# A graph layer on one core: setup, end of the kernel, order of the one-hots and shares of the gather changed

## The chip, the core and the metric

The kernel runs on one core of a Trainium2 chip. The core has TensorE (PE; its weight loads are shown apart as PEld), VectorE (DVE), ScalarE (ACT), GpSimd (POOL) and SyncE (SP), each with an instruction stream of its own that is worked off in order, and 16 DMA engines that all of them feed. The metric is the time of one execution on the device in microseconds (us); lower is better. Before the change the median of three runs is 1567.36 us (1563.31 to 1572.13).

## The reference

A layer of a graph network: 6250 nodes with 64 features, 200,000 edges sorted by destination.

```python
w = silu(edge_attr @ W1 + b1) @ W2 + b2              # (E,32)@(32,64), then @(64,9)
h_src = features[src]                                # a row of x for every edge
msg = einsum('ef,em,fmg->eg', h_src, edge_sh * w, W_tp)   # f=64, m=9, g=64
agg = segment_sum(msg, dst, num_segments=N) / sqrt(16)
emb = silu(c_noise[:, None] @ Wn1 + bn1) @ Wn2 + bn2
gamma, beta = split(emb, 2, axis=-1)
x = layernorm(x + agg * (1.0 + gamma) + beta)
```

All in float32.

## The kernel before

Edges are cut into 1563 tiles of 128 (one edge to a partition), the tiles into 98 groups of 16 (`KB`; the last has 11). The nodes make 49 columns of 128 (`NJ`).

**Rows of x for the edges.** A tile's 128 rows of x come in one of three ways. Most tiles are gathered by GpSimd, one indirect DMA a tile (`gather`, L91), into `hs`, of which there are seven buffers (`AHEAD` + 1). The last three or four tiles of each group are "picked" on TensorE (`pick`, L463 to L486): x lies in SBUF as two parts (`xs`, a rounded one and the rest) in 7 x 128 rows of 7 nodes; `hots` (L460, VectorE) makes a one-hot matrix of the tile's keys, `hot_k`, and 14 matmuls of 128 x 448 (L475) choose blocks of seven rows into `px` (two buffers); two VectorE operations (`xm`, L484 and L486) choose the row out of the seven. `picked(g)` says how many of a group are picked: 355 in all. The keys are worked out once in the setup on VectorE, transposed, written to DRAM (`kd`), and loaded for two groups at a time spread over all partitions (`load_keys`, `kr`, L391); `keys` (L454, ScalarE) puts them into PSUM. In every sixth group from 7 (`SPG`, 16 groups) the first tile's rows are loaded by SyncE one row at a time (`load_rows`, L101 and L106): it reads 8 row numbers into registers and issues 8 DMAs of 256 bytes, 22 rows (`SPR`) in a turn, beginning six turns ahead.

**Messages.** For each group `hidden` (L403, L411) and `second` (L420, L423) are the two layers on the edge attributes, `weights` (L430 to L442) forms `a`, the weights spread over a window of eight nodes. `windows` (L504, L514) multiplies the rows of x with `a` per tile into sums for eight nodes; `project` (L543, L546, L549) multiplies them by `W_tp` for a pair of groups; `place` (L559) puts them on node columns with a one-hot matrix, adding the part that the column before carried over (`carry`, `yt`); `bring` (L576) transposes two columns, and `finish` does the residual, the scale and shift and the layer norm (L669 to L682) and stores them (L683). `gate` (L589, L355, L356) makes the scale and the shift of one column a turn, up to turn 50.

**The order** is written out by hand (`tc.manual_schedule`); each engine keeps the order in which the program issues. A turn i of the main loop works on several groups at once: it gathers group i + 6, loads edge data and keys, issues SyncE's rows, makes the one-hots of group i + 2 (`hots(i + 2, 0, 2)`, then `hots(i + 2, 2, Q)`), picks the first tile of group i + 1 with the parts of `nodes(i)` (gate, place or bring, finish) put between its matmuls, then `hidden(i + 2)`, `second(i + 1)`, `windows(i)`, `project` in odd turns, and the other picks of group i + 1. `nodes(i)` and `second(i + 1)` share one PSUM buffer (tag `s`), so L420 of `second` must wait until everything of `nodes` is read. `project` and `hidden` share another (tag `p1`), so L543 waits until the Silu of L411 has read it. `finish` is in every fourth turn from turn 7 and needs a square root on ScalarE (L679), which loads another function table than Silu's.

**Setup** loads the indices and x, works out the keys of all groups, writes `kd` and reads it back, splits x into `xs` (`between` puts other work between the seven parts; each part goes through PSUM), spreads the first destination of every tile over the partitions with matmuls (`base`) and begins groups 0 and 1. **The end**: after the last turns the last pair and the last single group go through project, place, bring and finish separately.

Of the kernel before, what the change touches and what calls it, by code (L numbers as in the profile page):

```python
# [30 lines left out]
SPG = range(7, NBLK, 6)  # L31
SPR = 22
# [17 lines left out]
def picked(g):  # L50

    return Q - (3 * g % 8 < 3)
# [7 lines left out]
def gnn_resnorm_kernel(ctx: ExitStack, tc: tile.TileContext, x, src, dst, dst_row, ea, sh, cn,  # L60
# [18 lines left out]
    with ExitStack() as fast:  # L79
# [18 lines left out]
        def load_rows(g, e0):  # L98
            for e in range(e0, min(e0 + SPR, P), 8):
                n = min(8, min(e0 + SPR, P) - e)  # L100
                _, vs = nc.values_load_multi_w_load_instructions(  # L101
                    src_r[SPG.index(g):SPG.index(g) + 1, e:e + n], engines=[mybir.EngineType.SP],
                    min_val=0, max_val=NPAD - 1,
                    skip_runtime_bounds_check_because="src is below N, as for the gathers")
                for k in range(n):
                    nc.sync.dma_start(hs[g][e + k:e + k + 1, 0, :], x[bass.ds(vs[k], 1), :])  # L106
# [19 lines left out]
        kd = dram.tile([C, P], F16, name="kd")  # L126
        cn_d = dram.tile([P, NJ], F32, name="cn_d")
# [6 lines left out]
        def setup(temp):  # L134
# [7 lines left out]
            xb_r = xb.rearrange("p j f -> p (j f)")  # L142
            row_i = xb_r[0:1, 0:NBLK * KB].bitcast(I32)
            nc.scalar.dma_start(row_i, dst[0:1, :])
            first_i = temp.tile([NBLK, KB], I32)
            nc.scalar.dma_start(first_i, dst[0].rearrange("(g k) -> g k", k=KB))
            cn_j = temp.tile([NJ, P], F32)
            nc.scalar.dma_start(cn_j, cn)
            for s in range(2):
                nc.scalar.dma_start(b1c[s * H:(s + 1) * H, :], b1.unsqueeze(1))  # L150
# [3 lines left out]
            for h0, h1 in ((0, 2), (2, 4), (4, 7)):  # L154
                nc.scalar.dma_start(xk[:, h0:h1, :], x_v[:, h0:h1, :])
            load(0)
            for s in range(2):
                nc.sync.dma_start(w2p[s * H:(s + 1) * H, s * M:(s + 1) * M], w2)
            nc.sync.dma_start(dst_i, dst)

# [17 lines left out]
            row_f = xb_r[0:1, NBLK * KB:2 * NBLK * KB]  # L178
            nc.scalar.copy(row_f, row_i)
# [7 lines left out]
            nc.vector.tensor_add(ident2, ident[:, 0:F], ident[:, F:P])  # L187
            zero = temp.tile([P, 1], F32)
            nc.vector.memset(zero, 0.0)
            for k in range(2):  # L190
                nc.vector.memset(ht[k][H:H + 1], 1.0)
            nc.vector.memset(wtc2[F:P, 4], 0.0)
            ones1 = temp.tile([1, P], F32)
            nc.vector.memset(ones1, 1.0)
# [7 lines left out]
            s_f, kp, kh, rest, t0, t1 = [zt_r[:, k * C:(k + 1) * C] for k in range(6)]  # L202
            ti = [t.bitcast(I32) for t in (t0, t1)]
            s_f = s_f.rearrange("p (g k) -> p g k", k=Q)
            nc.vector.tensor_copy(s_f[:, 0:NBLK - 1, :],
                                  src_i.rearrange("p (g k) -> p g k", k=KB)[:, 0:NBLK - 1, KB - Q:])
            nc.vector.tensor_copy(s_f[:, NBLK - 1, :], src_i[:, NT - Q:NT])
            s_f = s_f.rearrange("p g k -> p (g k)")
            nc.vector.tensor_scalar(ti[0], s_f, 2675.0, None, op0=ALU.mult)
            nc.vector.tensor_scalar(ti[0], ti[0], 17, None, op0=ALU.logical_shift_right)  # L210
            nc.vector.tensor_copy(kp, ti[0])
            nc.vector.scalar_tensor_tensor(rest, kp, -float(J * J), s_f, op0=ALU.mult, op1=ALU.add)
            nc.vector.tensor_scalar(ti[1], rest, 37.0, None, op0=ALU.mult)
            nc.vector.tensor_scalar(ti[1], ti[1], 8, None, op0=ALU.logical_shift_right)
            nc.vector.tensor_scalar(kh, ti[1], float(P), None, op0=ALU.mult)
            kf = s_f
            nc.vector.tensor_add(kf, kp, kh)
            for c0 in range(0, C, P):
                n = min(P, C - c0)
                p_kt = psum.tile([P, P], F32, tag=("s", "r")[c0 // P % 2], name=f"p_kt{c0}")  # L220
                nc.tensor.transpose(p_kt[0:n], kf[:, c0:c0 + n], ident)
                kt = t1[:, c0 // 2:c0 // 2 + P // 2].bitcast(F16)
                nc.scalar.copy(kt[0:n], p_kt[0:n])
                nc.sync.dma_start(kd[c0:c0 + n, :], kt[0:n])
            nc.vector.scalar_tensor_tensor(jl, kh, -float(J) / P, rest, op0=ALU.mult, op1=ALU.add)
            hidden(0, act=False)
            load_keys(0)
            load_keys(LB)
# [4 lines left out]


            rel_v = rel.rearrange("p (a b c) -> p a b c", a=2, b=2)
            dst_v = dst_i.rearrange("p (a b c) -> p a b c", a=2, b=2)
            row_v = row_f.rearrange("p (a b c) -> p a b c", a=2, b=2)

            def base(a_):
                p_b = psum.tile([P, 2, KB * P // 4], F32, tag="p1", name=f"p_b{a_}")  # L240
                for b_ in range(2):
                    nc.tensor.matmul(p_b[:, b_, 0:NBLK * KB // 4], ones1, row_v[:, a_, b_, :], start=True, stop=True)
                nc.vector.tensor_sub(rel_v[:, a_], dst_v[:, a_], p_b[:, :, 0:NBLK * KB // 4])
# [17 lines left out]
            def between(h):  # L261

                if h == 0:
                    p_f = psum.tile([KB, NBLK], F32, tag="s", name="p_f")
                    nc.tensor.matmul(p_f, first_t, ident[0:NBLK, 0:NBLK], start=True, stop=True)
                    nc.scalar.copy(first_f, p_f)
                elif h == 1:
                    keys(0)
                    hots(0, 0, Q)
                elif h == 3:  # L270
                    p_cn = psum.tile([P, NJ], F32, tag="s", name="p_cn")
                    nc.tensor.matmul(p_cn, cn_j, ident[0:NJ, 0:NJ], start=True, stop=True)
                    cn_s = temp.tile([P, NJ], F32)
                    nc.scalar.copy(cn_s, p_cn)
                    nc.sync.dma_start(cn_d, cn_s)
                    nc.sync.dma_start(wn1c, wn1.rearrange("o h -> h o"))
                    nc.sync.dma_start(bn1c, bn1.unsqueeze(1))
                    gate_load(0)
                    nc.sync.dma_start(wn2a[0:H, :], wn2)
                    nc.sync.dma_start(wn2a[H:H + 1, :], bn2.unsqueeze(0))  # L280
                    for q in range(2):
                        n = (M + 1 - q) // 2
                        nc.sync.dma_start(wtc2[q * F:(q + 1) * F, 0:n, :], wtp[:, q:M:2, :])
                    load(LB)
                    with nc.allow_non_contiguous_dma(reason="2048 words, once"):
                        nc.sync.dma_start(src_r, src[:, SPG[0] * KB:NBLK * KB:6 * KB].rearrange("p g -> g p"))


            for h in range(J):
                xh = gam[:, h * J:(h + 1) * J, :].rearrange("p l f -> p f l")  # L290
                xp = psum.tile([P, F, J], F32, tag="px" if h in (2, 3) else "pz", name=f"x{h}", bufs=2)
                nc.scalar.copy(xp, xh)
                nc.scalar.copy(xs[0][:, h], xh)
                nc.vector.tensor_sub(xs[1][:, h], xp, xs[0][:, h].bitcast(F32))  # L294
                if h == 1:
                    hidden_act(0)
                between(h)
            pick(0, 0)
            keys(1)
            hots(1, 0, Q)  # L300
            base(0)
            near(0)
            second(0)
            pick(0, 1)
            base(1)

# [3 lines left out]
            for f in weights(0):  # L310
                f()
            ids()
            hidden(1)
            nc.scalar.copy(zt[F:P, :, 4].rearrange("p a k w -> p a (k w)"),
                           zero[F:P, :, None].to_broadcast([F, 4, P]))
            for t in range(2, Q):
                pick(0, t)
# [41 lines left out]

        def finish(j0, j1, sums):  # L360
            y = late.tile([P, j1 - j0, F], F32, tag="y", name=f"y{j0}")
            finish_nodes(nc, late, eps, sums, y, gam[:, j0:j1, :], xb[:, j0:j1, :], out_v[:, j0:j1, :], j0)
# [25 lines left out]
        def load_keys(g):  # L388
# [3 lines left out]
                              rows(kd[g * Q:(g + n) * Q, :].rearrange("c e -> (c e)"), P))  # L392
# [101 lines left out]
        def windows(g):  # L494
# [4 lines left out]
            for k0 in range(0, nk, ZT):  # L499
# [12 lines left out]
                for v in range(2):  # L512
                    for h in range(2):
                        nc.scalar.copy(  # L514
# [15 lines left out]
        def project(q):  # L530
# [3 lines left out]
            pt = psum.tile([P, 2, 4 * P], F32, tag="p1", name=f"pt{q}")  # L534
            z = [zs.pop(g).rearrange("p c k w -> p c (k w)") for g in gs]
            if len(gs) == 1:
                for c in range(5):
                    nc.tensor.matmul(pt[:, 0, 0:F], z[0][:, c], wtc2[:, c, :], start=(c == 0), stop=(c == 4))
                halves(q, pt[:, 0, 0:F].unsqueeze(1))
                return []  # L540
            for c in range(5):
# [12 lines left out]
        def place(q, pd):  # L554
# [3 lines left out]
            def part(k):  # L558
                nc.tensor.matmul(pd, r[q][:, k].rearrange("p s f -> p (s f)"), hot.pop(gs[k]),  # L559
                                 start=(k == 0), stop=(k == len(gs) - 1))  # L560
                if k == len(gs) - 1:
                    r.pop(q)
                    if q > 0:
                        yt[q - 1] = work.tile([P, P], F32, tag="yt", name=f"yt{q}", bufs=3)
                        nc.vector.tensor_add(yt[q - 1], pd[:, 0:P], carry.pop(q - 1))  # L565
# [34 lines left out]
        with tc.manual_schedule(), tc.tile_pool(name="temp", bufs=1) as temp:  # L600
            setup(temp)

            for i in range(NBLK):
# [34 lines left out]
                if i == NBLK - 1:  # L638
                    for f in turn:
                        f()  # L640
# [217 lines left out]
```

## Time and profile before

| | us |
|---|---|
| median of three runs | 1567.36 |
| the profiled execution, its own time | 1570.09 |
| its span | 1568.3 |
| TensorE busy | 1460.5 |
| VectorE busy | 1139.5 |
| GpSimd busy (0.3 us between its gathers not counted) | 1129.5 |
| ScalarE busy | 528.6 |
| first window matmul | 55.8 |
| last window matmul | 1551.9 |

Busy times are sums over the span; a line of a group names the line of the kernel, the engine, the operation, what is written from what, the count, then busy time, mean nanoseconds of one, and the idle time of that engine just before with what ended it. A line in order of time gives start and duration, and in brackets the wait just before it and what ended that. A line of a window gives busy time and count of PE, PEld, DVE, ACT and POOL, then the granted clock of TensorE as a share of full speed, the busy share of the DMA engines and GB/s.

### The profile page before, as it was taken

The page shows a single profiled execution, that of the slowest core. Times are in us where ns is not written, and L with a number is a line of the kernel's source. Part 1 is how long each engine was busy: PE and PEld are TensorE (multiplying, and loading weights), DVE is VectorE, ACT ScalarE, POOL GpSimd, SP SyncE. Part 2 cuts the span into 40 slices and gives each one's busy share as a digit, 9 for nine tenths or more (in the row PEclk, how much of TensorE's full clock was granted, in tenths as well). Part 3 has the DMA queues.
Part 4 walks back from the last instruction along what each step waited for, and adds up shares of the span by engine and source line. Part 5 has one row for each costly group of instructions (what it writes and reads, how often), then busy time and mean ns, then how long its engine had stood idle before and what let it go on. Part 6 is the DMA issues. An engine that isn't in the chain of part 4 may idle for free.

```text
span 1568.3 us, 34363 instructions
## 1 busy us (share of the span) xinstructions
PE 1460.5 (93%) x10810; PEld 1208.6 (77%) x10810; DVE 1139.5 (73%) x1987; ACT 528.6 (34%) x1335; POOL 1129.5 (72%) x1201
## 2 busy tenths in 40 slices
PE   4998999999999999999999999999999999999995
PEld 2787778778787788787877877877877878778774
DVE  5686777777777777777777777777777677777773
ACT  4232242433332423332333323323233332333331
POOL 7777777777777777777777777777777777777700
PEclk9999999999999999999999999999999999999997
DMA  5321222222222222222222222222222222222200
GB/s 166 93 62 55 53 75 51 63 56 71 57 62 65 63 54 61 56 71 59 58 71 53 59 53 71 59 53 70 53 60 55 68 54 58 71 53 59 71 7 5
DMA packets 90939, 96.16 MB, mean 61 GB/s; under 512 B 37161, under 2 KB 51451, under 8 KB 90748
## 3 DMA queue, kind: packets, MB, share of 16 engines
q1 hardware_dynamic: 51842, 53.09, 11.5%
q0 software_dynamic: 38144, 39.14, 11.4%
q8 instruction: 88, 1.44, 0.4%
q10 hardware_dynamic: 762, 1.64, 0.3%
q14 instruction: 103, 0.84, 0.2%
HBM read 92.04 MB, written 1.73 MB: 60 GB/s over the span
## 4 chain that ended last, share of the span: by engine, by line
PE 51%; POOL 20%; DVE 13%; issue 8%; DMA 4%; ACT 3%; SPq 0%; DVEq 0%; POOLq 0%; ACTq 0%
PE px L475 37%; POOL hs L91 20%; DVE hot_k L460 5%; PE pz L504 5%; DMA hs<-in_x_dram,src_i 4%; PE pt L543 3%; PE p L420 2%; DVE xm L484 2%; DVE hs L486 2%; PE p L403 1%; PE p L430 1%; ACT L411 1%; ACT st L411 1%; DVE oh L382 1%; ACT carry L568 1%
## 5 line engine op out<-in xcount | busy, mean ns | idle before, releaser
L91 POOL DMA_INDIRECT hs<-in_x_dram,src_i x1192 | 1128.2, 946 | 364.0 <-issue 335.0
L475 PE MATMUL px<-xs,hot_k 128*128 128x448 f32 x4970 | 1100.8, 375 | 8.4 <-DVE xs L294 7.8
L475 PEld LDWEIGHTS px<-xs,hot_k 128*128 128x128 f32 x4970 | 903.3, 190 | 96.7 <-issue 12.2
L484 DVE SCALAR_TENSOR_TENSOR xm<-li,jl,px 128x448 f32<-128x448 f32 x355 | 240.4, 677 | 220.2 <-PE px L475 217.9
L460 DVE TENSOR_TENSOR hot_k<-pk,nk 128x896 fp32r<-128x896 f32 x355 | 370.5, 1081 | 2.3 <-ACT pk L454 2.3
L486 DVE TENSOR_REDUCE hs<-xm 128x64 f32<-128x448 f32 x355 | 220.1, 620 | 12.5 <-DVE xm L484 0.2
L514 ACT COPY zt<-pz 64x160 f32<-64x160 f32 (+2 forms) x784 | 213.3, 272 | 23.0 <-PE pz L504 13.9
L411 ACT ACTIVATE st<-p,b1c 128x1024 f32<-128x1024 f32 x98 | 109.2, 1114 | 296.1 <-PE p L403 295.8
L568 ACT COPY carry<-ps 128x128 f32<-128x128 f32 x48 | 12.7, 265 | 390.2 <-DVE yt L565 382.4
L436 DVE TENSOR_TENSOR p<-p,sh 128x72 f32<-128x72 f32 x196 | 47.3, 241 | 132.7 <-ACT rt L546 47.7
L504 PEld LDWEIGHTS pz<-a,hs 128*64 128x64 f32 x3126 | 110.6, 142 | 41.9 <-issue 38.4
L442 DVE TENSOR_TENSOR a<-oh,p 128x1152 f32<-128x1152 f32 x98 | 132.6, 1353 | 3.3
L504 PE MATMUL pz<-a,hs 128*64 128x72 f32 x3126 | 125.5, 236 | 1.1 <-DMA hs<-in_x_dram,src_i 0.6
L403 PE MATMUL p<-ea,w1bd 64*128 64x512 f32 x392 | 113.5, 656 | 0.0
L420 PEld LDWEIGHTS p<-st,w2p 128*32 128x32 f32 x784 | 16.6, 108 | 113.3 <-issue 52.7
L543 PE MATMUL pt<-zt,wtc 128*64 128x128 f32 x960 | 72.8, 305 | 27.7 <-ACT st L411 26.0
L420 PE MATMUL p<-st,w2p 128*32 128x256 f32 x784 | 63.7, 395 | 35.7 <-DVE xb L356 32.0
L543 PEld LDWEIGHTS pt<-zt,wtc 128*64 128x64 f32 x960 | 62.2, 157 | 29.7 <-ACT st L411 27.8
L679 ACT ACTIVATE var<-var,eps 128x2 f32<-128x2 f32 (+1 forms) x25 | 7.4, 296 | 220.5 <-DVE var L678 220.5
L430 PE MATMUL p<-ident,p2s 128*128 128x128 f32 x196 | 54.4, 278 | 0.0
L454 ACT CAST pk<-kr 128x384 f32<-128x384 f16 (+1 forms) x98 | 53.9, 550 | 1.5 <-DMA kr<-kd 1.4
L403 PEld LDWEIGHTS p<-ea,w1bd 64*128 64x128 f32 x392 | 30.2, 188 | 28.8 <-issue 27.9
(122 smaller groups left out, 530.0 us busy)
## 6 DMA issues: line engine op xcount, KB each, us to landing
hs<-in_x_dram SPq DMA_DIRECT2D x2048, 0.2 KB
ea<-in_ea_dram SPq DMA_DIRECT2D x49, 512.0 KB
hs<-in_x_dram,src_i POOLq DMA_INDIRECT x1192
kr<-kd SPq DMA_DIRECT2D x49, 256.0 KB
sh<-in_sh_dram SPq DMA_DIRECT2D x49, 144.0 KB
cb<-cn_d SPq DMA_DIRECT2D x12, 128.0 KB
out_dram<-o SPq DMA_DIRECT2D x24, 64.0 KB
gam<-in_x_dram ACTq DMA_DIRECT2D x2, 448.0 KB
```

The costliest lines, as they stand in the source:

```text
L91: hs_dma[g] = [nc.gpsimd.indirect_dma_start(out=hs[g][:, t - g * KB, :], out_offset=None, in_=x, in_offset=bass.IndirectOffsetOnAxis(ap=sr ...
L403: nc.tensor.matmul(p1[:, i, :], w1bd[i * 64:(i + 1) * 64, :], e[i * 64:(i + 1) * 64, :], start=True, stop=True)
L411: nc.scalar.activation(st[g], p1_t.pop(g), AF.Silu, bias=b1c)
L420: nc.tensor.matmul(p2[g][c * D:(c + 1) * D, 0, :].rearrange("p (i e) -> p i e", i=2), w2p, s[:, :, c * P:(c + 1) * P], start=True, stop=True)
L442: nc.vector.tensor_mul(a[g], oh_t.pop(g)[:, :, None, :].to_broadcast([P, KB, M, W]), sw.unsqueeze(3).to_broadcast([P, KB, M, W]))
L460: nc.vector.tensor_tensor(hot_k[g, t], pk_t[g][:, t, None, :].to_broadcast([P, J, P]), nk.unsqueeze(2).to_broadcast([P, J, P]), op=ALU.is_ ...
L475: nc.tensor.matmul(px.rearrange("p f l -> p (f l)"), hot_k[g, t][:, h, :], xs[i][:, h].rearrange("p f l -> p (f l)"), start=(h == 0 and i ...
L484: nc.vector.scalar_tensor_tensor(xm, li[:, None, :].to_broadcast([P, F, J]), jl[:, c:c + 1], px, op0=ALU.is_equal, op1=ALU.mult)
L486: nc.vector.tensor_reduce(hs[g][:, tiles(g) - q + t, :], xm, AX.X, ALU.add)
L504: mm = nc.tensor.matmul(pz[v * F:(v + 1) * F, k // 2].rearrange("p m w -> p (m w)"), hsg[:, k0 + k, :], ag[:, k0 + k].rearrange("p m w -> ...
L514: nc.scalar.copy(z[h * F:(h + 1) * F, 0:5 - h, k0 + v:k0 + n:2, :].rearrange("p m k w -> p k m w"), pz[v * F:(v + 1) * F, 0:(n + 1 - v) // ...
L543: nc.tensor.matmul(pt[h * F:(h + 1) * F, 0, 0:P], wtc2[:, c, :], z[h][:, c], start=(c == 0), stop=(c == 4))
```

## The change

Eight edits:

- The setup works out and stores the keys of the first two groups alone first (`key_rows(0, LB)`, stored to `kd_0`), and those of the other 96 after two picks of group 0 (`key_rows(LB, NBLK)`).
- x is rounded and split straight from SBUF (`split`), not through PSUM, and its loads are issued ahead of two small ones.
- The first destination of each tile comes to all partitions by one DMA of 128 equal rows (`row_i`), not by one row, a cast and matmuls; `rel` is a subtraction of two SBUF tiles. The other small loads of the setup move behind the picks of group 0.
- In a turn, the first two one-hots of group i + 2 are issued behind the parts of `nodes(i)`, still between the matmuls of the first pick (`more`).
- Picked tiles: one fewer in every third group (359 in all), not in three of eight (355).
- SyncE's rows: every fifth group (19 tiles), 26 rows a turn in batches of 13.
- A store of `finish` is issued at the head of the next turn; in `place` the carry copy is issued ahead of the addition; a single group's `project` uses the PSUM tag `r`.
- The end: windows of the last group go in reverse order, half of the copies of the last two groups go to VectorE, and the last pair and the last single group share one `place`, one `bring` and one `finish` of three columns.

```diff
-SPG = range(7, NBLK, 6)
-SPR = 22
+SPG = range(7, NBLK, 5)
+SPR = 26
...
-    return Q - (3 * g % 8 < 3)
+    return Q - (g % 3 == 0)
...
-            for e in range(e0, min(e0 + SPR, P), 8):
-                n = min(8, min(e0 + SPR, P) - e)
+            for e in range(e0, min(e0 + SPR, P), SPR // 2):
+                n = min(SPR // 2, min(e0 + SPR, P) - e)
...
+            row_i = xb.rearrange("p j f -> p (j f)")[:, 0:NBLK * KB].bitcast(I32)
+            nc.sync.dma_start(row_i, rows(dst[0, :], P))
...
+            key_rows(0, LB)
+            load_keys(0)
             hidden(0, act=False)
-            load_keys(0)
-            load_keys(LB)
...
+            def split(h):
                 xh = gam[:, h * J:(h + 1) * J, :].rearrange("p l f -> p f l")
-                xp = psum.tile([P, F, J], F32, tag="px" if h in (2, 3) else "pz", name=f"x{h}", bufs=2)
-                nc.scalar.copy(xp, xh)
                 nc.scalar.copy(xs[0][:, h], xh)
-                nc.vector.tensor_sub(xs[1][:, h], xp, xs[0][:, h].bitcast(F32))
-                if h == 1:
-                    hidden_act(0)
-                between(h)
+                nc.vector.tensor_sub(xs[1][:, h], xh, xs[0][:, h].bitcast(F32))
+
+            for h in range(2):
+                split(h)
+            hidden_act(0)
+            keys(0)
+            hots(0, 0, Q)
+            for h in range(2, J):
+                split(h)
+            load(LB)
+
+            nc.vector.tensor_sub(rel[:, 0:2 * KB], dst_i[:, 0:2 * KB], row_i[:, 0:2 * KB])
+            near(0)
+            keys(1)
             pick(0, 0)
-            keys(1)
-            hots(1, 0, Q)
-            base(0)
-            near(0)
+            hots(1, 0, 2)
             second(0)
             pick(0, 1)
-            base(1)
-
+            for f in weights(0):
+                f()
+            key_rows(LB, NBLK)
+            load_keys(LB)
+            hots(1, 2, Q)
+            hidden(1)
+            for t in range(2, Q):
+                pick(0, t)
+            nc.vector.tensor_sub(rel[:, 2 * KB:], dst_i[:, 2 * KB:], row_i[:, 2 * KB:])
...
+            loads_late()
             ids()
-            hidden(1)
-            for t in range(2, Q):
-                pick(0, t)
...
                 if i + 2 < NBLK:
                     keys(i + 2)
-                    hots(i + 2, 0, 2)
-                pick(i + 1, 0, [nodes(i)])
+                    more = [lambda: hots(i + 2, 0, 2)]
+                pick(i + 1, 0, [nodes(i), more])
...
-                        nc.scalar.copy(
+                        (nc.vector.tensor_copy if v and g >= NBLK - 2 else nc.scalar.copy)(
...
+            turn = project(NBLK // 2 - 1)
             project(NBLK // 2)
+            for f in turn:
+                f()
+            ps = psum.tile([P, 2 * P], F32, tag="s", name="ps_n")
+            py = psum.tile([P, 3, F], F32, tag="r", name="py_n")
+            for f in place(NBLK // 2 - 1, ps, NBLK // 2) + bring(NJ - 3, NJ, py):
                 f()
```

`key_rows(g0, g1)` has the arithmetic that the setup had for all groups at once, on the columns of groups g0 to g1, with its transposes, copies and stores.

## The prediction

> **What bounds the kernel now.** I read the page's shares first, then TensorE's waits, then one loop turn in order of time, then the granted clock, then GpSimd's and SyncE's groups. The page:
>
> ```profile
> span 1568.3 us, 34363 instructions
> PE 1460.5 (93%) x10810; PEld 1208.6 (77%) x10810; DVE 1139.5 (73%) x1987; ACT 528.6 (34%) x1335; POOL 1129.5 (72%) x1201
> ...
> L91 POOL DMA_INDIRECT hs<-in_x_dram,src_i x1192 | 1128.2, 946 | 364.0 <-issue 335.0
> ```
>
> TensorE is busy for 93%. GpSimd's 72% hides a second bound: the gathers follow one another every 0.95 + 0.30 = 1.25 us, "issue" being no wait. From the tile view of hs, 1192 gathers from 2.9 to 1493.2 us make 1.251 us each: GpSimd never stops. Counting gathers against the starts of the window matmuls (L504), each group's last gather is done 32 us (group 3) to 56 us (groups 44 and 97) before TensorE needs it. So TensorE sets the pace, 15.33 us a turn (windows of turn 8 at 183.9, of turn 95 at 1517.2), with GpSimd close behind at 1192/98 x 1.251 = 15.22. The chain's 20% for GpSimd is an artefact: its DMA pieces lie beside ordinary 0.30 us issue gaps. What makes TensorE wait:
>
> ```profile
> PE p L420 <- DVE xb L356: 32.0, 34, 2.2
> PE pt L543 <- ACT st L411: 26.0, 12, 2.2
> ```
>
> Columns: us, times, longest. These two are nearly all the idle time of turns 0 to 95. Their cause, in turn 27 (in order of time: start, duration):
>
> ```profile
> 472.86 2.08 DVE L460 TENSOR_TENSOR hot_k<-pk,nk 128x896 fp32r<-128x896 f32 x2
> ...
> 473.08 0.33 PE L576 MATMUL ps<-ident,yt 128*128 128x64 f32 x2
> ...
> 474.86 0.28 DVE L669 TENSOR_TENSOR y<-ps,gam 128x128 f32<-128x128 f32 x1
> 475.00 1.13 PE L403 MATMUL p<-ea,w1bd 64*128 64x512 f32 x4
> ...
> 477.87 0.21 DVE L356 TENSOR_TENSOR xb<-xb,ps 128x64 f32<-128x64 f32 x1
> ...
> 478.23 0.64 PE L420 MATMUL p<-st,w2p 128*32 128x256 f32 x8 [2.10 <-DVE xb L356]
> ```
>
> The sums of two output columns are in PSUM at 473.41; VectorE takes them at 474.86, as two hot_k stand before them; the last reader of that bank (L356) ends at 478.08, and L420, which needs the bank, has waited 2.10 us. Then the clock:
>
> ```profile
> 479.60:483.00 3.40, 3.40 (x36) 3.03 (x33) 1.72 (x2) 2.81 (x11) 2.77 (x3) 0.50 0.63 218
> 1215.00:1276.00 61.00, 60.20 (x444) 50.11 (x444) 43.63 (x73) 18.79 (x53) 46.05 (x50) 0.97 0.23 59
> ```
>
> The seventh figure is the granted clock: 0.50 from 479.6 to 483.0. I found 14 such stretches between 168 and 1525 us, each beginning 2.0 to 3.8 us after the start of a stall of 2.1 to 2.2 us; 9 of the 23 such stalls had none, and no stall of 0.4 us had one. Turn 24 (half clock at 418.2) took 15.41 us, turn 16, of the same pattern but none, 13.77: one costs 1.63 us.
>
> **The change, part by part** (against the profiled execution: span 1568.3, its own time 1570.09, so 1.8 outside; the median 1567.36 is 2.7 lower).
>
> (1) First two hot_k of group i+2 behind the node work (`more`). In finishing turns (every fourth, from 7) VectorE takes the sums at about 473.6, just after TensorE wrote them, 1.26 us earlier; the chain to L356 (3.22 us) ends at 476.8, and TensorE, ready at 476.13, waits 0.8 in place of 2.1: 11 x 1.3 = 14.4. Late next are the hot_k (wanted a turn later) and xm, 1.1 us later, where VectorE had 2.7 us idle before the next L436; px has two buffers and hot_k seven, so nothing on TensorE waits. Without that cover each finishing turn pays about 1 us, 24 in all. In other turns the 0.38 waits (23) and 0.15 waits on carry (22) go: 8.8 + 3.3. From turn 51 on no gate follows, and the stall is L543 on the Silu that stands behind Sqrt and its table load; these start 1.9 us earlier (mul at 1513.75 for 1515.64), so 2.17 becomes 0.25: 12 x 1.9 = 23. Sum -49.5. Ends: -24 if half goes, -58 if all of the 32.0 + 26.0 goes.
>
> (2) The half-clock stretches follow those stalls: 14 x 1.63 = -22.8. Ends: 0 and that. The row that decides is the 0.4 us stalls with none: the remaining 0.8 and 0.25 are nearer to them than to 2.1. The Trainium skill ("TensorE: Matmul & The Clock Gate", section "Why this matters for your kernels") says the clock halves after an idle gap above about 3 us. By that these stretches, behind gaps of 2.1 us, would not come from the stalls and would stay, and the sum would be 22.8 higher; the trace has them only behind the stalls, and I go by it.
>
> (3) Picks 355 to 359. Picks follow one another every 2.89 us (xm at 1506.61, 1509.50, 1512.39): +11.6 on TensorE, and four gathers less on GpSimd.
>
> (4) Three more tiles by SyncE: 7 gathers less with (3), 8.8 us on GpSimd, which then ends at 2.9 + 1185 x 1.251 = 1485.3, the last one landed 2.4 later. Nothing on TensorE as long as SyncE keeps up. Its rows:
>
> ```profile
> L101 SPq TENSOR_LOAD <-src_r x288: 690/995/2097, 50.8 to 1529.9; - x144
> ...
> 463.52 10.86 SPq L106 DMA_DIRECT2D hs<-in_x_dram  x22
> ...
> SPq L683 <- DVE o L682: 69.0, 14, 21.9
> SPq L106 <- PE pz L504: 47.3, 15, 5.1
> ```
>
> 22 rows with two register loads inside (0.78 and 0.98) take 10.86, so 0.41 a row. A turn now has 25.6 rows in two batches: 10.5, two loads of 0.7 to 1.9 (2.7), other DMAs 1.2: 14.4 us, before 13.5. It fits under 14.6 to 15.1, with little to spare. A load of 13 words is not in the trace: those of 2 words took 0.73 and those of 8 at least 0.69, so I take no dearer ones; the upper end is rival D. The stores move to the head of the next turn, which is the same place in SyncE's queue: 0.
>
> (5) Setup. Before, the keys reach PSUM at 21.46 (ACT L454) and the first windows start at 55.84. After, the x copies through PSUM go (7 x 0.9 on ScalarE) and ScalarE's issue of x comes 2.3 us earlier. But the early keys' store (8 columns, ready near 7 us) stands in SyncE's queue behind dst and a new 128-row load of dst (0.8 MB each), and dst itself must wait for the semaphore of the last x load: keys at 20.5 (18 to 22). From there hots 3.1, five splits 3.2, xm and two hots 3.4, the second pick on a cold clock 5.3, weights 1.9, then the other groups' key arithmetic (10 operations, 4.9 us, on VectorE between 7.9 and 13 us before) with TensorE waiting for its transposes; then transposes, L403, the third pick, three small matmuls with copies between: windows of group 0 at 57, between 50 and 63. So +1 (-6 to +7).
>
> (6) The end. Before, 25.8 us from windows of group 96 (1542.5) to the end. Now that group's and the last one's windows follow each other, half of their copies go to VectorE, and one place, one bring and one finish serve three columns: windows 2.5, copies 1.0, L543 and L538 2.6, halves 1.9, place and bring 2.2, finish of ten operations 3.7, and 5.9 from the last o to the end as before: about 19. -7 (-3 to -9).
>
> (7) Where the paces meet. TensorE without stalls needs 15.33 - 0.56 - 0.25 + 0.12 = 14.65 a turn, GpSimd 1185/98 x 1.251 = 15.13. The lead of 32 us shrinks by 0.5 a turn; with the leads of the trace it is 13 us at group 60 and gone near 80, after which TensorE follows the gathers: about +5 (0 to +10). This also swallows most of what the setup wins or loses.
>
> Sum: 1568.3 - 49.5 - 22.8 + 11.6 + 1 - 7 + 5 = 1506.6 of span, 1508 with what lies outside; the floor is the last gather landed at 1487.7 plus some 15. I allow 2 us for waits at the meeting paces that the even sum does not see, and leave the median's 2.7 aside: 1510.
>
> **Rivals.**
> A, the stalls shrink but half-clock stretches stay (gather waits of 1 to 2 us could bring new ones): TensorE then meets no gathers, 1510 - 5 - 2 + 22.8 = 1526. For it: 0.8 us stalls were never seen; against: (2).
> B, VectorE becomes the pace: its 1002.75 us busy in 88 turns is 11.4 a turn, with 0.03 between its 20 instructions 12.0, and it now waits in order for place and bring. If one pick a turn then waits 0.3, TensorE needs 97 x 0.3 = 29 more, of which 9 are waited anyway: 1530. Against it: 218 us in which it waited for px.
> C, GpSimd was the pace all along, as the chain's 20% says: then only 7 gathers and the end count, 1568.3 - 8.8 - 7 = 1553. Against it: leads of 32 to 56 us.
> D, slower: SyncE's queue becomes the pace. If a register load grows with its words, from the mean of 1.36 for 8 to 2.2 for 13, a turn is 10.5 + 4.4 + 1.2 = 16.1, and the windows of group 96 come at 57 + 96 x 16.1 = 1603, the end 19 later and 1.8 outside: 1624. It decides from 15.6 a turn (1575). Against it: the 2-word loads took as long as the shortest 8-word ones.
> E, no change: setup and gains cancel against picks within 0.5%.
>
> **How the numbers follow.** Forecast 0.60, A 0.17, B 0.07, C 0.05, D 0.08, E 0.03. Within 0.5% (8 us) is what a measurement of this kernel can hardly tell from no change. Faster: 0.60 + 0.17 + 0.07 + 0.05 = 0.89; same 0.03; slower 0.08. The range runs from 1500 (floor) to 1545, which holds the forecast, A and B with their spread, about 0.82.
>
> **What would show it.** Right: L420's wait on xb falls from 32.0 to near 9 us and L543's on st from 26.0 to near 3; the granted clock has at most a few 0.50 stretches after 150 us; GpSimd's last gather issues near 1484; TensorE's waits on hs grow from nothing late in the span; windows of group 0 near 57; less than 20 us from the windows of group 96 to the end. Wrong: half-clock stretches with stalls below 1 us (A), TensorE waiting for xm (B), gather waits from the first turns (C), matmuls waiting for ea or kr, with no wait left on SyncE's stores (D).

## The result and the profile after

The changed kernel takes 1709.87 us (median of four runs, 1708.81 to 1712.36); the kernel before took 1569.74 us beside it (four runs). The ratio is 1.0893, with a 95% interval of 1.0841 to 1.0946: slower by 8.9%, where 1510 us was forecast. In five of the seven sets of experiments (e1 to e4, e9 to e16, e18) the kernel before itself took 2.54 to 2.58 ms in place of 1.57, and the traces of the altered kernels there have VectorE idle for 524 to 638 us ahead of xm for no releaser that they show, so those sets are read for the durations of their register loads alone.

The page of the changed kernel (first lines, the chain that ended last, GpSimd's group):

```profile
span 1708.8 us, 35535 instructions
PE 1493.6 (87%) x10858; PEld 1216.3 (71%) x10858; DVE 1149.3 (67%) x2006; ACT 519.7 (30%) x1318; POOL 1124.8 (66%) x1194
...
SPq 55%; PE 17%; issue 16%; DMA 4%; POOL 4%; DVE 3%; ACT 1%; DVEq 0%; ACTq 0%
SPq L106 32%; SPq L101 20%; PE px L469 11%; POOL hs L91 4%; DMA ea<-in_ea_dram 3%; PE pz L499 2%; PE p L397 1%; PE p L414 1%; SPq L367 1%; PE pt L539 1%; SPq L365 1%; DMA hs<-in_x_dram,src_i 1%; SPq L385 1%; DVE xm L478 1%; DVE hot_k L454 1%
...
L91 POOL DMA_INDIRECT hs<-in_x_dram,src_i x1185 | 1123.5, 948 | 467.6 <-issue 320.2
```

The chain now runs through SyncE's queue: 32% of the span are the row DMAs (L106), 20% the register loads ahead of them (L101, which read row numbers from `src_r` in SBUF into SyncE's registers), and "issue" lies between them. From the windows of turn 8 to those of turn 95 a turn of the loop takes 16.74 us, before 15.33. TensorE's waits (us, times, longest):

```profile
PE p L397 <- DMA ea<-in_ea_dram: 159.3, 43, 16.0
...
PE p L414 <- DVE xb L347: 7.8, 11, 0.9
...
PE pt L539 <- ACT st L405: 1.8, 11, 0.2
```

The two stalls that the prediction named are gone as it said (they were 32.0 and 26.0). A new wait stands in their place: edge data for two groups (`ea`) is loaded in every second turn, its DMA is issued by SyncE behind the rows, and it comes late nearly every time. In order of time (start, duration):

```profile
469.72 0.41 SPq L356 DMA_DIRECT2D out_dram<-o  x1
470.19 0.46 SPq L365 DMA_DIRECT2D ea<-in_ea_dram  x1
470.70 0.46 SPq L367 DMA_DIRECT2D sh<-in_sh_dram  x1
474.27 12.70 SPq L106 DMA_DIRECT2D hs<-in_x_dram  x23
...
474.47 2.08 PE L397 MATMUL p<-ea,w1bd 64*128 64x512 f32 x4 [5.92 <-DMA ea<-in_ea_dram]
```

TensorE waits 5.92 us for what SyncE issued at 470.19. Between the issue of sh (done 471.16) and the next rows (474.27) SyncE does nothing but one register load, of 2.87 us. Windows of the changed kernel around this wait (length; busy time and count of PE, PEld, DVE, ACT, POOL; granted clock; DMA share; GB/s):

```profile
463.00:468.00 5.00, 5.00 (x29) 4.69 (x28) 4.48 (x13) 0.27 (x1) 3.78 (x5) 1.00 0.14 27
472.80:479.40 6.60, 4.93 (x44) 2.62 (x44) 0.25 (x1) 2.11 (x5) 3.98 (x5) 0.50 0.33 97
480.00:485.00 5.00, 5.00 (x28) 4.59 (x27) 3.14 (x5) 1.40 (x5) 3.78 (x5) 1.00 0.13 25
```

The wait is paid twice: once as idle time, and once in the 6.8 us at half clock (0.50) that begin 4.1 us into it.

**Where the loads' time was to be seen.** All loads of one turn, from the line view of L101 (minimum, median, maximum in ns, first and last start). First the kernel before, four turns of one tile with 8, 8 and 6 words each:

```profile
L101 SPq TENSOR_LOAD <-src_r x3: 782/974/983, 521.2 to 534.1; - x3
L101 SPq TENSOR_LOAD <-src_r x3: 1535/1865/1934, 543.5 to 554.1; - x3
L101 SPq TENSOR_LOAD <-src_r x3: 722/807/982, 558.6 to 566.9; - x3
L101 SPq TENSOR_LOAD <-src_r x3: 1540/1863/1926, 571.8 to 582.4; - x3
```

Then the changed kernel, one load to a line, those that begin at word 0, 13, 26, 52 and 65 of the row:

```profile
L101 SPq TENSOR_LOAD <-src_r x1: 1157/1157/1157, 503.5 to 503.5; - x1
L101 SPq TENSOR_LOAD <-src_r x1: 2923/2923/2923, 510.8 to 510.8; - x1
L101 SPq TENSOR_LOAD <-src_r x1: 3128/3128/3128, 520.2 to 520.2; - x1
L101 SPq TENSOR_LOAD <-src_r x1: 1179/1179/1179, 538.9 to 538.9; - x1
L101 SPq TENSOR_LOAD <-src_r x1: 2943/2943/2943, 545.6 to 545.6; - x1
```

Before, the turns alternate. With 22 rows a turn each turn begins 88 bytes further on, so every second one begins off a multiple of 16 bytes, and there the loads of 8 words take 1.9 us in place of 0.8 and those of 6 take 1.5 in place of 1.0. In the changed kernel, batches of 13 begin on a multiple of 16 bytes at words 0, 52 and 104 alone: these loads take 1.2 us, and six of the seven others 2.9 (the last one, of 11 words, 2.5). All 190 loads take 455 us, 4.79 for each of the 95 turns that have rows; the prediction had 2.7.

### The profile page after: what moved, and what is told of

It is laid out like the page before. It is cut to its first block, busy times and chain, and to the rows that moved or that the text cites. A ratio compares the mean times of both kernels' runs of the same rounds, so it can differ in the third digit from the quotient of the medians.

```text
span 1708.8 us, 35535 instructions
## 1 busy us (share of the span) xinstructions
PE 1493.6 (87%) x10858; PEld 1216.3 (71%) x10858; DVE 1149.3 (67%) x2006; ACT 519.7 (30%) x1318; POOL 1124.8 (66%) x1194
## 3 DMA queue, kind: packets, MB, share of 16 engines
q8 instruction: 88, 1.44, 0.3%
## 4 chain that ended last, share of the span: by engine, by line
SPq 55%; PE 17%; issue 16%; DMA 4%; POOL 4%; DVE 3%; ACT 1%; DVEq 0%; ACTq 0%
SPq L106 32%; SPq L101 20%; PE px L469 11%; POOL hs L91 4%; DMA ea<-in_ea_dram 3%; PE pz L499 2%; PE p L397 1%; PE p L414 1%; SPq L367 1%; PE pt L539 1%; SPq L365 1%; DMA hs<-in_x_dram,src_i 1%; SPq L385 1%; DVE xm L478 1%; DVE hot_k L454 1%
## 5 line engine op out<-in xcount | busy, mean ns | idle before, releaser
L397 PE MATMUL p<-ea,w1bd 64*128 64x512 f32 x392 | 134.6, 769 | 159.4 <-DMA ea<-in_ea_dram 159.3
L509 ACT COPY zt<-pz 64x160 f32<-64x160 f32 (+1 forms) x776 | 211.7, 273 | 35.8 <-PE pz L499 27.3
L499 PEld LDWEIGHTS pz<-a,hs 128*64 128x64 f32 x3126 | 123.3, 155 | 53.7 <-issue 48.7
L499 PE MATMUL pz<-a,hs 128*64 128x72 f32 x3126 | 138.6, 250 | 2.7 <-DVE zt L509 1.2
L414 PE MATMUL p<-st,w2p 128*32 128x256 f32 x784 | 75.0, 460 | 7.8 <-DVE xb L347 7.8
L539 PE MATMUL pt<-zt,wtc 128*64 128x128 f32 x960 | 61.3, 274 | 1.9 <-ACT st L405 1.8
L448 ACT CAST pk<-kr 128x512 f32<-128x512 f16 (+1 forms) x98 | 54.2, 553 | 14.7 <-DMA kr<-kd 14.7
L539 PEld LDWEIGHTS pt<-zt,wtc 128*64 128x64 f32 x960 | 51.8, 137 | 3.7 <-ACT st L405 3.7
```

What stands on the lines that cost most here:

```text
L397: nc.tensor.matmul(p1[:, i, :], w1bd[i * 64:(i + 1) * 64, :], e[i * 64:(i + 1) * 64, :], start=True, stop=True)
L499: mm = nc.tensor.matmul(pz[v * F:(v + 1) * F, k // 2].rearrange("p m w -> p (m w)"), hsg[:, k0 + k, :], ag[:, k0 + k].rearrange("p m w -> ...
L509: (nc.vector.tensor_copy if v and g >= NBLK - 2 else nc.scalar.copy)(z[h * F:(h + 1) * F, 0:5 - h, k0 + v:k0 + n:2, :].rearrange("p m k w ...
L539: nc.tensor.matmul(pt[h * F:(h + 1) * F, 0, 0:P], wtc2[:, c, :], z[h][:, c], start=(c == 0), stop=(c == 4))
```

## The experiments

Theory L, from here on, says that a load's duration is set by where its words begin. "On a line" means that the first word lies on a multiple of 16 bytes in SBUF, "off a line" that it doesn't. By theory L four words of a load that begins on a line cost as much as one word of a load that begins off it.

**Line starts: the changed kernel, each batch of 13 on a line of its own** (e1, e5):

```diff
-        src_r = keep.tile([len(SPG), P], I32)
+        src_r = keep.tile([len(SPG), 10 * 16], I32)
...
-                    src_r[SPG.index(g):SPG.index(g) + 1, e:e + n], engines=[mybir.EngineType.SP],
+                    src_r[SPG.index(g):SPG.index(g) + 1, e // 13 * 16:e // 13 * 16 + n], engines=[mybir.EngineType.SP],
...
-                    nc.sync.dma_start(src_r, src[:, SPG[0] * KB:NBLK * KB:5 * KB].rearrange("p g -> g p"))
+                    s_r = src[:, SPG[0] * KB:NBLK * KB:5 * KB].rearrange("p g -> g p")
+                    for e in range(0, P, 13):
+                        n = min(13, P - e)
+                        nc.sync.dma_start(src_r[:, e // 13 * 16:e // 13 * 16 + n], s_r[:, e:e + n])
```

> The changed kernel, with one thing altered: the row numbers of each batch of 13 begin on a 64-byte line of their own in SBUF (ten small loads in the setup in place of one); same loads, same 13 words, same rows. Theory L (what makes a register load dear is where its words begin: 0.33 us + 0.20 us for each access, an access being four words inside a 16-byte line when the load begins on such a line, and a single word when it doesn't; this makes the 13-word loads of the changed kernel 1.19 and 2.94 us): every load 1.2 us, a SyncE turn 10.55 + 2 x 1.2 + 1.2 = 14.1 us in place of 16.6, below TensorE's 14.65; TensorE's wait on ea, 159 us, gone; 1514 us (1505 to 1530). Rival W (a load is dear by its number of words, wherever they begin): loads stay at 2.9 us in the median, 1700 to 1712 us. Rival S (25.6 rows a turn are too many for SyncE whatever the loads take, or the stores' new place holds it up): loads get cheap and the time stays above 1600 us.

> The kernel of e1_line_starts again, since the kernel before took 2583 us beside it in place of 1570, with TensorE waiting for xm for 500 us, so that SyncE bound nothing; the loads of 13 words took 1.18 us there, whatever their number in the row, which speaks for theory L (a load is dear by where its words begin) and against W (by its number of words). With the kernel before near 1570 us. Theory L: SyncE's turn 14.1 us, TensorE's wait on ea gone, 1514 us (1505 to 1530). Rival S (25.6 rows a turn, or the stores' new place, hold SyncE up whatever the loads take): above 1600 us.

Measured, e5: 1518.26 us (1517.39 to 1520.1), ratio 0.9702 (0.9653 to 0.9751). Its loads, and TensorE's first waits:

```profile
L101 SPq TENSOR_LOAD <-src_r x190: 1148/1226/1580, 85.4 to 1466.2; - x190
```

```profile
PE p L400 <- DMA ea<-in_ea_dram: 23.2, 2, 16.6
PE p_kt L220 <- DVE zt L216: 13.6, 2, 7.6
PE px L472 <- DVE hot_k L457: 8.7, 1, 8.7
PE p L417 <- DVE xb L350: 7.6, 11, 0.7
```

Same number of words, rows, tiles and loads as the changed kernel; only the place of the words in SBUF (and how they come there) differs. The loads fall to 1.23 us in the median and 2.50 a turn, a turn to 14.60 us, and 192 us of span go: 136 of the waits on ea, 55 of TensorE's busy time (1493.6 to 1438.9 for the same 10858 matmuls). Theory L holds; rivals W (the number of words) and S (the number of rows) fall. In e1, whose time is not read, the loads took 1.18 us as well.

**The rows undone, and the rows alone** (e2, e6: the changed kernel with the old rows; e3, e7: the kernel before with the new ones and its 355 picks). The edit of e6 (e7 has it the other way round, in the old kernel):

```diff
-SPG = range(7, NBLK, 5)
-SPR = 26
+SPG = range(7, NBLK, 6)
+SPR = 22
...
-            for e in range(e0, min(e0 + SPR, P), SPR // 2):
-                n = min(SPR // 2, min(e0 + SPR, P) - e)
+            for e in range(e0, min(e0 + SPR, P), 8):
+                n = min(8, min(e0 + SPR, P) - e)
...
-                    nc.sync.dma_start(src_r, src[:, SPG[0] * KB:NBLK * KB:5 * KB].rearrange("p g -> g p"))
+                    nc.sync.dma_start(src_r, src[:, SPG[0] * KB:NBLK * KB:6 * KB].rearrange("p g -> g p"))
```

> The changed kernel with the rows of 19 tiles undone: 16 tiles by SyncE, 22 rows a turn in loads of 8, as before; everything else changed. Theory L and rivals W and S: SyncE's turn is back at 13.5 us, 1520 us (1508 to 1535), which is what the other parts of the change are worth (-49.5 - 22.8 + 11.6 + 1 - 3 against before, with three more gathers for GpSimd). Rival O (another part is the cause: the edge-data load stands late because of the setup or the stores' place): stays above 1600 us.

> The kernel of e2_rows_undone again (16 tiles by SyncE, 22 rows a turn in loads of 8, everything else as changed), beside a kernel before near 1570 us. Theory L and rival S: SyncE's turn back at 13.5 us, 1520 us (1508 to 1535), the worth of the other parts of the change. Rival O (another part is the cause): above 1600 us.

> The kernel before with only the rows changed: 19 tiles by SyncE, 26 rows a turn in two loads of 13; 355 picks, old setup, old order of hots, old end, stores in their old place. Theory L, rivals W and S: SyncE's turn is 16.6 us and sets the pace from the start, 56 + 96 x 16.7 + 26 = 1685 to 1730 us, with TensorE waiting for ea. Rival O: near 1565 us.

> The kernel of e3_rows_alone again (the kernel before with 19 tiles by SyncE in loads of 13, nothing else), beside a kernel before near 1570 us. Theory L and rival S: SyncE's turn is 16.6 us and sets the pace, 1685 to 1730 us, with TensorE waiting for ea. Rival O: near 1565 us.

Measured: e6 1514.21 us (1513.97 to 1515.09), ratio 0.9677 (0.9628 to 0.9725); e7 1693.65 us (1690.82 to 1696.64), ratio 1.0828 (1.0772 to 1.0883). Waits in the trace of e6, then in that of e7:

```profile
PE pz L499 <- DMA hs<-in_x_dram,src_i: 9.4, 5, 3.2
PE p L414 <- DVE xb L347: 7.9, 11, 0.8
PE p L397 <- DMA ea<-in_ea_dram: 7.1, 1, 7.1
```

```profile
PE p L403 <- DMA ea<-in_ea_dram: 90.2, 36, 5.7
PE pt L543 <- ACT st L411: 25.9, 12, 2.2
PE p L420 <- DVE xb L356: 25.1, 16, 2.3
```

The rows alone make the kernel before 8% slower, with a turn of 16.74 us like the changed kernel's; without them the rest of the change makes it 3.2% faster. Rival O (another part of the change is the cause) falls from both sides.

**Words shifted by one: 16 tiles and loads of 8, 8 and 6 as in e6, the row numbers 4 bytes further** (e11, e12, e15, e17):

```diff
-        src_r = keep.tile([len(SPG), P], I32)
+        src_r = keep.tile([len(SPG), P + 4], I32)
...
-                    src_r[SPG.index(g):SPG.index(g) + 1, e:e + n], engines=[mybir.EngineType.SP],
+                    src_r[SPG.index(g):SPG.index(g) + 1, 1 + e:1 + e + n], engines=[mybir.EngineType.SP],
...
-                    nc.sync.dma_start(src_r, src[:, SPG[0] * KB:NBLK * KB:6 * KB].rearrange("p g -> g p"))
+                    nc.sync.dma_start(src_r[:, 1:P + 1], src[:, SPG[0] * KB:NBLK * KB:6 * KB].rearrange("p g -> g p"))
```

> The kernel of e6_rows_undone (16 tiles, 22 rows a turn in loads of 8, 8 and 6) with the row numbers laid one word further in SBUF, and nothing else: now every load begins off a 16-byte line. Theory L: all loads of 8 words take 1.9 us and those of 6 1.5 (half of them took 0.73 to 0.99), a SyncE turn is 21.3 x 0.412 + 5.26 + 1.2 = 15.3 to 15.5 us, above TensorE's 14.8, so SyncE becomes the pace: 59 + 96 x 15.4 + 22 = 1560 us (1540 to 1580), with waits on ea from the first third on. Rival W (the duration goes with the number of words or the place in the turn): loads as in e6_rows_undone, 1514 us.

> The kernel of e11_words_shifted again, since the kernel before took 2579 us beside it and SyncE bound nothing; the loads of 8 words took 1.87 us there, as theory L has it, and not the 0.73 of half of them at their old place. Beside a kernel before near 1570 us. Theory L: SyncE's turn 15.3 to 15.5 us against TensorE's 14.8, so SyncE becomes the pace: 1560 us (1540 to 1580), waits on ea from the first third on. Rival M (a load's place in SBUF sets its duration but not the kernel's time; the changed kernel's loss is in the number of rows): 1514 us, as e6_rows_undone.

> The kernel of e12_words_shifted once more (16 tiles, loads of 8, 8 and 6, row numbers one word further in SBUF). Beside a kernel before near 1570 us. Theory L: SyncE's turn 15.3 to 15.5 us against TensorE's 14.8: 1560 us (1540 to 1580), waits on ea from the first third on. Rival M (the place of the words sets the load's duration but not the kernel's time): 1514 us, as e6_rows_undone.

> The kernel of e15_words_shifted (16 tiles, loads of 8, 8 and 6, row numbers one word further). Beside a kernel before near 1570 us. Theory L: SyncE's turn 15.3 to 15.5 us against TensorE's 14.8: 1560 us (1540 to 1580), waits on ea from the first third on. Rival M: 1514 us, as e6_rows_undone.

Measured, e17: 1578.51 us (1578.29 to 1578.86), ratio 1.0084 (1.0053 to 1.0114); e11, e12 and e15 are not read for time; their loads of 8 words took 1.87 to 1.88 us in the median. All loads of three turns of e17, and its first wait:

```profile
L101 SPq TENSOR_LOAD <-src_r x3: 1543/1922/2123, 537.1 to 548.3; - x3
L101 SPq TENSOR_LOAD <-src_r x3: 1525/1887/1928, 554.2 to 564.9; - x3
L101 SPq TENSOR_LOAD <-src_r x3: 1521/1867/1928, 569.4 to 580.0; - x3
```

```profile
PE p L397 <- DMA ea<-in_ea_dram: 51.1, 25, 4.3
```

Four bytes cost 64 us against e6, which ran in another set; the kernel before took 1564.79 us beside e17 and 1568.19 beside e6. Loads take 5.28 us a turn, up from 3.86 in the kernel before, and a turn 15.42, up from e6's 14.78: SyncE is now the pace, by little. Rival M (the place sets the duration but not the time) falls. The time is 18 us above the middle of what was expected, though inside its range, and so is the turn; the stretches at half clock (11 after the first 100 us, against 5 in e6) had not been counted. TensorE is busy for 24.3 us more than in e6 (1463.5 against 1439.2) with the same matmuls.

**Line starts, with the hots in their old place** (e4, e8): as e5, and

```diff
-                    more = [lambda: hots(i + 2, 0, 2)]
-                pick(i + 1, 0, [nodes(i), more])
+                    hots(i + 2, 0, 2)
+                pick(i + 1, 0, [nodes(i)])
```

> As the first of this set (13-word loads beginning on lines of their own), but the first two hot_k of group i+2 again ahead of pick(i+1, 0) and the node work. If steps (1) and (2) of the prediction hold (stalls of 2.2 us behind the node work, and half-clock stretches behind them): 49.5 + 22.8 us come back, less some 7 us as GpSimd is no longer met: 1575 us (1560 to 1590), L414 waiting on xb 30 us or more, L539 on st 20 us or more, and 10 to 16 half-clock stretches. Rival G (with SyncE out of the way GpSimd's gathers set the pace and the order of VectorE's work is worth nothing): within 10 us of the first of this set.

> The kernel of e4_lines_hots_first again (line starts, but the first two hot_k ahead of the node work), beside a kernel before near 1570 us. If steps (1) and (2) of the prediction hold: 1575 us (1560 to 1590), the wait on xb 30 us or more, that on st 20 us or more, 10 to 16 half-clock stretches. Rival G (with SyncE out of the way GpSimd's gathers set the pace, and the order of VectorE's work is worth nothing): within 10 us of the kernel with line starts.

Measured, e8: 1575.55 us (1573.39 to 1577.4), ratio 1.005 (1.002 to 1.0079), 57 us above e5. The waits that come back:

```profile
PE pt L542 <- ACT st L408: 25.8, 12, 2.2
PE p L417 <- DVE xb L350: 23.3, 11, 2.2
```

Of the 57.3 us of span 39.7 are these two waits (49.1 against 9.4 in e5) and 17.0 TensorE's busy time (1455.9 against 1438.9), with 10 stretches at half clock after 100 us against 2. Rival G (the order of VectorE's work is worth nothing) falls. The wait on xb is 23.3 us, not the 30 expected: the 23 small ones among the 34 of before did not come back, so they belong to another part of the change.

**Loads of 16 and 12 words, with 359 and with 355 picks** (e9, e13, e16, e18; e10, e14). Edit: `SPR = 28`, loads of at most 16 words; for the second kernel also `Q - (3 * g % 8 < 3)` in `picked`.

> The changed kernel with 28 rows a turn in loads of 16 and 12 words, so that every load begins on a 16-byte line without any other layout (0, 16, 28, 44, ... words); 19 tiles and 359 picks as changed. It takes the ten small setup loads of the earlier kernel with line starts (16.7 us of SyncE's queue, and one wait on ea of 16.6 us behind them) out again. Theory L: loads of 1.1 and 0.9 us (four and three accesses), a SyncE turn of 13.8 in the mean; 1518 less the 16.6 us wait would be 1501, but GpSimd's 1185 gathers at 1.251 us then hold the end: its last gather lands near 1489, and the last windows stood 8.5 us after that; 1509 us (1504 to 1516). Rival W2 (16 words cost more than 13 wherever they begin, or 28 rows in most turns are too many): 1530 us or more, TensorE waiting for ea again.

> As the kernel with loads of 16 and 12 words, but 355 picks as before (four picks fewer on TensorE, 11.6 us; four gathers more on GpSimd, 5.0 us). Theory F (GpSimd's gathers are the floor, as step (7) of the prediction had it): not faster, 0 to 5 us slower than with 359 picks, 1509 to 1514 us, TensorE waiting for hs. Rival T (TensorE still sets the pace): 1497 to 1500 us.

> The kernel of e9_batches_16_12 again, beside a kernel before near 1570 us. Theory L: loads of 1.2 and 0.9 us, SyncE's turn 13.9 us, the 16.6 us wait behind the ten small setup loads gone, GpSimd's gathers holding the end: 1509 us (1504 to 1516). Rival W2 (28 rows in most turns are too many for SyncE): 1530 us or more, TensorE waiting for ea again.

> The kernel of e10_batches_355_picks again, beside a kernel before near 1570 us. Theory F (GpSimd's gathers are the floor): 0 to 5 us slower than e13_batches_16_12, TensorE waiting for hs. Rival T (TensorE sets the pace): 8 to 12 us faster than it.

> The kernel of e13_batches_16_12 once more (19 tiles, loads of 16 and 12 words, each beginning on a 16-byte line). Beside a kernel before near 1570 us. Theory L: SyncE's turn 13.9 us, GpSimd's gathers holding the end: 1509 us (1504 to 1516). Rival W2: 1530 us or more, TensorE waiting for ea again.

> The kernel of e16_batches_16_12 (19 tiles, loads of 16 and 12 words, each beginning on a 16-byte line). Beside a kernel before near 1570 us. Theory L: SyncE's turn 13.9 us, GpSimd's gathers holding the end: 1509 us (1504 to 1516), 5 us less than with 16 tiles (1514). Rival W2 (28 rows in most turns are too many for SyncE): 1530 us or more, TensorE waiting for ea again.

None of these six can be read for time, so what 28 rows a turn cost, and theories F and T (whether the gathers or TensorE hold the end), stay open. Their loads bear out L: medians of 1.18 us for 16 words and 0.92 to 1.00 for 12, below the 1.9 of 8 shifted ones.

The expectation of e9 also holds an error that the traces show: it laid the 16.6 us wait of e5 on that kernel's ten small setup loads. The changed kernel, with its one load, has that wait too (the 16.0 above). SyncE's queue in the setup, first of the changed kernel, then of e6:

```profile
58.43 0.46 SPq L265 DMA_DIRECT2D src_r<-in_src_dram  x1
59.20 15.32 SPq L309 DMA_DIRECT2D xb<-in_x_dram  x1
```

```profile
58.46 1.16 SPq L265 DMA_DIRECT2D src_r<-in_src_dram  x1
59.83 0.89 SPq L309 DMA_DIRECT2D xb<-in_x_dram  x1
```

With 2432 single words ahead of it, the load of xb holds the queue for 15.32 us; with 2048 (e6) for 0.89. The edge data of group 4 is issued at 99.1 in place of 82.4, and TensorE waits 16.0. So 19 tiles cost some 16 us in the setup. On line starts a turn of the loop is shorter with them (14.60 us in e5 against 14.78 in e6, 15.1 us over 87 turns), and e5 is 4 us slower than e6. How much of the shorter turn the three tiles bring is not shown: e5 enters turn 8 at 203.7 us, 19 us later than e6, and TensorE then waits 0.4 us for gathers where e6 waits 9.4, so a part of it may be no more than the later start. That the wait in the setup would go if this load stood elsewhere was not tried.

## Why the prediction was wrong

**Step (4) failed: "two loads of 0.7 to 1.9 (2.7)" are 4.79 us.** With the measured price its own sum gives 10.5 + 4.8 + 1.2 = 16.5 a turn (measured 16.74), over its own limit of 14.6 to 15.1. "A load of 13 words is not in the trace: those of 2 words took 0.73 and those of 8 at least 0.69, so I take no dearer ones" took the shortest loads of 8 for the price of a word count. The row had a minimum of 690, a median of 995 and a maximum of 2097 ns, and the spread was no noise: laid out by turns, it alternates. Off a line a load of 8 took 1.9 and one of 2 0.73, that is 0.20 a word, which makes 2.9 for 13; seven of ten of the new batches begin off a line. With 2.5 us for the loads (e5) the sum is 14.2, and SyncE does fit. The step also put at nothing what a longer list of row numbers costs in the setup; there TensorE waits 16.0 us.

The Trainium skill ("Runtime: NRT & Kernel Launch", section "Instruction fetch mechanics") gives about 200 ns for each register, even in bulk, and the page speaks of registers loaded from HBM. The slope off a line here, from SBUF, is 0.20 us a word, and on a line these runs have four words for that price. An estimate from that page, 13 x 0.2 = 2.6 us, lies above the 2.2 of rival D; measured were 2.4 in the mean.

**Rival D had the path, with a wrong reason, and was priced too low.** SyncE's queue did become the pace. But D had a load grow with its words, and loads of the same 13 words take 1.2 us on a line and 2.9 off it. It took loads of 2.2 where they are 2.4 in the mean, had no wait in the setup (16 us) and no stretches at half clock, so it said 1624. Its threshold was near: e17 stands at 15.42 us a turn and 1578.5 us, where D put 15.6 and 1575. "Against it: the 2-word loads took as long as the shortest 8-word ones" was true, and a sign of the mechanism: those 2 words lay off a line and those 8 on it.

**Step (1) held in the main.** The waits are 7.8 and 1.8 (9 and 3 were forecast), and no pick in the loop waits for hot_k behind them. The 8.8 us for the 0.38 waits came too, but e8 shows that the order of the one-hots is not what brings them. Steps (1) and (2) together are worth 57 us by e8 against e5; the forecast was 49.5 + 22.8, less some 7 for GpSimd, and the 8.8 in it are not among those 57.

**Step (2) held where no new stalls came** (e5: 2 stretches after 100 us, 21.2 us in all; before: 16, 77.0 us), and the changed kernel shows its converse: 27 stretches, 156.2 us.

**Steps (5) to (7).** Windows of group 0 begin at 57.9 (57). Keys reach PSUM at 21.7 (20.5). From the windows of group 96 to the end it takes 22.9 us (19), and 20.6 to 21.0 in e6 and e5, so -4.8 to -5.2 against 25.8, not -7. The last gather ends at 1487.2 in e5 (1485.3); TensorE waits 9.4 us for gathers in e6, 0.4 in e5 (5 was forecast). Step (3) was never measured alone.

**The sum held without step (4)**: e6 has a span of 1512.2 and a time of 1514.2, with the 1188 gathers that 16 tiles leave; forecast 1506.6 and 1510. In e6 the setup (first windows at 58.9 in place of 55.8), the end (-5.2) and the waits for gathers (9.4) each cost 2 to 4 us more than forecast; the picks were not measured. Both e6 and e5 beat either kernel.

## What to carry to other kernels

When a row's shortest and longest instruction differ threefold, find what separates them, by time and by address, before a new size is priced from either end. An in-order queue that feeds the engine that sets the pace has a limit of its own: sum it with measured prices, and where it comes within one instruction's spread of the limit, the forecast has to allow for both outcomes. Lay out words that go to registers in batches that begin on multiples of 16 bytes.

## What the runs showed of the hardware that was not expected

- A register load from SBUF by its first word's place (medians for each place in e5, e6, e7 and e17; words: us). On a line 8: 0.73 to 0.80, 6: 0.99, 13: 1.18 to 1.25, 11: 1.44. Off it 2: 0.73, 6: 1.53 to 1.54, 8: 1.88 to 1.94, 11: 2.54, 13: 2.94 to 2.96. All lie within 0.12 of 0.33 + 0.20 for each four words on a line, for each single word left over, and for each word of a load that begins off a line. That the load reads in such steps is argued from this fit, not shown.
- The time for which SyncE's next DMA is held behind a scattered load: 15.3 us behind 2432 single words (8.7 in e7, where that DMA came 8.8 us after it), 0.8 to 1.0 behind 2048 (before, e6, e17). The cause was not looked for.
- TensorE's clock behind its idle stretches, counted after the first 100 us in the traces of before, after, e5 to e8 and e17 (a half-clock stretch that begins within 6.5 us of the start of the idle time): idle 0.3 to 1.5 us, 23 of 150; 1.5 to 2.5 us, 48 of 91; 2.5 to 3.5 us, 18 of 27; over 3.5 us, 40 of 40. A short wait alone is never followed by one: of the 99 of 0.3 to 1.5 us with no other wait beginning within 8 us, none is; of the 87 of 1.5 to 2.5 us that stand alone, 45 are. The Trainium skill ("TensorE: Matmul & The Clock Gate", section "Why this matters for your kernels") has the clock halve after gaps above about 3 us; the traces agree above 3.5, and show it behind half of those of 1.5 to 2.5 as well.
